# A cross-attention kernel's setup in another order: Wk's load and transposes first, batch 0's keys in pieces between the second attention's weights

## The chip, the cores and the metric

The kernel runs on one core of a Trainium2 chip. The metric is the device time in microseconds of one execution; three runs of the kernel before gave 958.2, 962.56 and 960.67, a median of 960.67. Profiles come from one further execution.

The engines are called PE (TensorE, matrix products), DVE (VectorE), ACT (ScalarE), POOL (GpSimd) and SP (SyncE, which here only issues DMAs). Each works through its own instructions in order. PE writes to PSUM, which ACT and DVE then copy to SBUF.

## What is computed

For each of 16 batches, `x` is 100 x 640 and the context is 722 x 384, of which the last four rows are the tokens `ca` and the other 718 are `enc`. There are 8 heads of 80.

```python
query = hidden_states @ Wq
keyt = enc @ Wk
valt = enc @ Wv
hs = _mha(query, keyt, valt)
ca_q1 = jnp.einsum('btc,th->bch', ca, Wq_ca)
ca_q1 = ca_q1[:, indices, :]
ca_hs1 = _mha(ca_q1, residual, residual)
ca_q2 = ca_hs1 @ Wq
ca_k2 = ca @ Wk_ca
ca_v2 = ca @ Wv_ca
ca_hs2 = _mha(ca_q2, ca_k2, ca_v2)
out = hs + ca_hs2
out = out @ Wout + b_out
out = out + residual
```

So there is a main attention over `enc`, and a second one over the four tokens whose queries come from yet another attention, of token channels over `x`. All is in 32-bit floats.

## The kernel before, in words

**The setup and the loop.** A setup loads and rearranges the weights and computes what batch 0 needs; then a loop runs over `b` in 0 to 15 (from the line `for b in range(B)`). In batch `b` the loop computes the scores of `b` (`scores`, L604), their softmax (the maxima at L1148 and L1136, `Maximum`, L1124, L1132), the values of `b` (`Values`, L425) and the keys of `b + 1` (`Keys`, L456), and at last the products of probabilities and values (L1283). From batch 1 on, keys and values come from a fast scheme with fewer products of 3 x 3 x 2 blocks, which needs sums of blocks of `enc` (`enc_sums`, on POOL, L491) and of the weights (`weight_sums`, L512). Batch 0's keys and four of its six blocks of values are computed plainly in the setup.

**The keys of batch 0.** The context's rows come in three thirds `u`, its 384 columns in three chunks `c`. `chunk_keys` (L549) computes one chunk `n` of 128 of the 640 key columns with 18 products over all thirds and chunks, and two copies by ACT (L560). `first_keys` does it for chunks 0 to 3 and then calls `last_keys` for chunk 4. The weights are Wk in rearranged columns, `wk_sb` (chunk 4: `wk4`). They are got by transposing `wkt_sb` on PE: for each `c`, three transposes into `w_ps_c` (L1037) and one copy by ACT (L1040). `wkt_sb` lies in the tile `kT`, and is loaded in five DMAs (L294), whose source `packed(wkt, c)` is 4 x 32 rows of 384 (8 x 16 for the last).

**The second attention's weights and first steps.** From `cat` and `wkca` come `k2_ps` (L991) and five masked copies (DVE, L1003); from these and the transposed Wq, `wqt` (L287, in the tile later used by Wout), the matrices `m_ps_c` (L1014), copied by DVE (L1022) to `m_sb`. `keys(load_m(b))` is five masked products on POOL (L702) into the tile `m2`. `second.products()` multiplies `m2` and `x` on PE (`y_ps`, L730) and reduces to `g` on DVE (L739). `second.scores1()` is seven POOL instructions of 100 x 800 (four products L765, three sums L772), which read `g`. `second.softmax1()` is their softmax on DVE (L656 to L686, L782); `exponentials1` is the exponential on ACT (L785). In batch 0 of the loop, `softmax1` comes ahead of the scores in DVE's order, and `exponentials1` comes between the first and the second scores' copies in ACT's order:

```python
        if b == 0:
            enc_sums(enc)
            now.load()
            now.softmax1()
        st.append(scores(b, 0, tiles))
        if b == 0:
            now.exponentials1()
        nc.vector.tensor_tensor(most[:KN], st[0][:, 0], st[0][:, 1], ALU.max)
        st.append(scores(b, 1, tiles))
        larger(1)
```

**Other pieces of the setup.** Wq is loaded in five chunks (L299) and rearranged by DVE with 15 copies (L1048, twice for each chunk, and L1055) into `wq_sb`, which the queries (L525) read. `weight_sums(nc.vector, w, False)` is seven subtractions on DVE for each of `wk_sb` and `wv_sb`; `weight_sums(nc.vector, wk_sb, True)` is five more, which overwrite raw weights and so come after batch 0's keys. `va_ps` (L1069) uses `wvca`, whose tile is the one that batch 1's `enc` is loaded to. Batch 1's `rest` is loaded to the tile that held `m_3`.

**What sets the order.** DMAs wrapped in `in_order` keep their program order on SP. From `tc.manual_schedule(engines=...)` on, every engine takes the instructions in the order of the program. Ahead of that call a planner orders each engine's instructions by its own costs, within the data's dependences; `tc.issue_after(ins)` puts a block's instructions behind a given one on its engine. In the kernel before, the call stands at the end of the setup, just ahead of the loop. So the setup is in the planner's order there, and its instructions can also stand between or behind those of the loop: Wout's load, of the loop, is issued at 38.15 us, and batch 1's `enc` at 56.05.

Of the kernel before, what the change touches and what calls it, by code (L numbers as in the profile page):

```python
# [15 lines left out]
NH, D = 8, 80  # L16
# [55 lines left out]
def packed(w, c):  # L72

    if c < 4:
        lo = (c // 2) * D + 32 * (c % 2)
        return w.rearrange("(r k) n -> r k n", r=RG)[:, lo : lo + 32]
    return w.rearrange("(h k) n -> h k n", h=NH)[:, 64:]
# [47 lines left out]
def kernel(  # L125
# [48 lines left out]
    def psum(name):  # L174

        turn[0] += 1
        return (psumk if turn[0] % 2 else psum1)(name)
# [17 lines left out]
    def vb_tile(name):  # L195
        return main.tile([P, T, H], F32, tag="vb", name=name)
# [46 lines left out]
    def in_order(dma):  # L243
        tc.keep_in_program_order(dma)
# [15 lines left out]
    def load_first(lo, hi, u, cols):  # L260

        for c in range(lo, hi):
            k = u * (KT - 1)
            in_order(
                nc.sync.dma_start(
                    out=a_raw(enc, u, c)[:, cols],
                    in_=enct[0][:, c, k + cols.start : k + cols.stop],
                )
            )
# [7 lines left out]
            )  # L277
    load_first(0, CC, 1, slice(KN, KT))
    load_first(0, CC, 2, slice(0, KT))
    tokens = vb_tile("tokens")  # L280
    cat_sb = tokens[:, CC, : CC * B * T].rearrange("p (c n) -> p c n", c=CC)
    wkca_sb = tokens[:, :CC, :]
    in_order(nc.sync.dma_start(out=cat_sb, in_=cat.rearrange("p c b t -> p c (b t)")))
    in_order(nc.sync.dma_start(out=wkca_sb, in_=wkca.rearrange("(c p) n -> p c n", p=P)))
    wqt_sb = wout_sb
    wkt_sb = kT.rearrange("p c u k -> p c (u k)")
    in_order(nc.sync.dma_start(out=wqt_sb, in_=wqt.rearrange("(c p) r -> p c r", p=P)))  # L287
    load_first(0, CC, 0, slice(0, KT))
    xT = inp.tile([P, 2, HC, S], F32, tag="xT", name="xT_0")
    in_order(nc.sync.dma_start(out=xT, in_=xt[0:2].rearrange("b p c s -> p b c s")))  # L290
    ca_0 = small.tile([S, T, S], F32, tag="ca", name="ca_0", bufs=2)
    in_order(nc.sync.dma_start(out=ca_0, in_=cas[0].unsqueeze(0).to_broadcast([S, T, S])))
    for c in range(HC):
        in_order(nc.sync.dma_start(out=wkt_sb[:, c, :CAD], in_=packed(wkt, c)))  # L294
    halves = [t[:, u] for t in [scores_tile(f"wq_{i}") for i in range(NP)] for u in range(2)]
    room = halves.pop()
    wq_in = [t[:, :H] for t in halves]
# [61 lines left out]
    def first_values(i, enc, engines, halves=(0, 1), get=psum):  # L359

        u, j = KC[i]
        for g in halves:
            engine = engines[g]
            v_ps = get(f"v_ps_0_{i}_{g}")
            for c in range(CC):
                nc.tensor.matmul(
                    v_ps[:KN, : H // 2],
                    a_raw(enc, u, c)[:, j * KN : (j + 1) * KN],
                    wv_sb[:, 2 * c + g],
                    start=(c == 0),  # L370
                    stop=(c == CC - 1),
                )
            engine(
                block(i, g)[:, :, :D],
                v_ps[:KN, : H // 2].rearrange("p (h d) -> p h d", d=D),
            )
# [167 lines left out]
    def chunk_keys(n, banks, weights, enc):  # L544
        copies = []
        for bank, thirds in zip(banks, ((0, 1), (2,))):
            for i, u in enumerate(thirds):
                for c in range(CC):
                    nc.tensor.matmul(  # L549
                        bank[:, i * KT : (i + 1) * KT],  # L550
                        weights[c],
                        a_raw(enc, u, c),
                        start=(i == 0 and c == 0),
                        stop=(c == CC - 1),
                        skip_group_check=True,
                    )
        for bank, thirds in zip(banks, ((0, 1), (2,))):
            w = len(thirds)
            copies.append(
                nc.scalar.copy(  # L560
                    kT[:, n, thirds[0] : thirds[0] + w],
                    bank[:, : w * KT].rearrange("p (u k) -> p u k", u=w),
                )
            )
        return copies

    def first_keys(enc):
        for n in range(HC - 1):
            banks = [psum(f"kT_ps_0_{n}_{k}") for k in range(2)]
            weights = [wk_sb[:, 2 * c + n % 2, n // 2] for c in range(CC)]  # L570
            chunk_keys(n, banks, weights, enc)
        last_keys(0, enc)

    def last_keys(b, enc):
        banks = pair(f"kT_ps_{b}")
        return chunk_keys(
            HC - 1,
            [banks[:, k] for k in range(2)],
            [wk4[:, c] for c in range(CC)],
            enc,  # L580
        )
# [106 lines left out]
    def load_m(b):  # L688
        if b < 2:
            return lambda c: m_sb[c][:, b * HT : (b + 1) * HT]  # L690
        mb = small.tile([P, HC, HT], F32, tag="mb", name=f"mb_{b}", bufs=2)
        nc.sync.dma_start(
            out=mb, in_=m_d[:, :, b * HT : (b + 1) * HT].rearrange("c p n -> p c n")
        )
        return lambda c: mb[:, c]
# [284 lines left out]
        nc.tensor.matmul(idle_ps[:, :P], idle, idle, start=True, stop=True)  # L980


    for i in (1, 4, 2, 5):
        first_values(i, enc, (act, dve))


    k2_ps = psum("k2_ps")
# [11 lines left out]
    for n, heads in enumerate(HEADS):  # L999
        cols = len(heads) * B * T  # L1000
        k2T.append(room[:, at : at + cols])
        at += cols
        nc.vector.tensor_tensor(  # L1003
            k2T[n].rearrange("p (h k) -> p h k", h=len(heads)),
            k2_ps[:, n * B * T : (n + 1) * B * T]
            .unsqueeze(1)
            .to_broadcast([P, len(heads), B * T]),
            hmask[:, n, : len(heads)].unsqueeze(2).to_broadcast([P, len(heads), B * T]),
            ALU.mult,
        )  # L1010
    for c in range(HC):
        m_ps = psum(f"m_ps_{c}")
        for n, heads in enumerate(HEADS):
            nc.tensor.matmul(  # L1014
                m_ps[:, heads[0] * B * T : (heads[-1] + 1) * B * T],
                wqt_sb[:, n, c * P : (c + 1) * P],
                k2T[n],
                start=(n == 0),
                stop=(n == HC - 1),
                skip_group_check=True,  # L1020
            )
        copied = nc.vector.tensor_copy(  # L1022
            m_sb[c].rearrange("p (b h t) -> p h b t", h=NH, t=T),
            m_ps.rearrange("p (h b t) -> p h b t", h=NH, b=B),
        )
        nc.sync.dma_start(out=m_d[c], in_=m_sb[c])
    second = Second(0, xT, ca_0)
    keys(load_m(0))
    summed = second.products()
    second.copy()  # L1030
    second.scores1()
    keys(load_m(1))

    for c in range(HC):
        w_ps = psum(f"w_ps_{c}")
        for cc in range(CC):
            nc.tensor.transpose(  # L1037
                w_ps[:, cc * P : (cc + 1) * P], wkt_sb[:, c, cc * P : (cc + 1) * P], ident
            )
        act(  # L1040
            wk_sb[:, c % 2 : 6 : 2, c // 2] if c < HC - 1 else wk4,
            w_ps[:, : CC * P].rearrange("p (a n) -> p a n", a=CC),
        )

    with tc.issue_after(summed.ins):
        for c in range(HC):
            for u in range(2):
                nc.vector.tensor_copy(  # L1048
                    wq_sb[:, c, 2 * u * P : 2 * (u + 1) * P].rearrange(
                        "p (a r k) -> p a r k", a=2, r=RG  # L1050
                    ),
                    wq_in[c].rearrange("p (r k) -> p r k", r=RG)[:, :, u * D : u * D + 64]
                    .rearrange("p r (a k) -> p a r k", a=2),
                )
            nc.vector.tensor_copy(  # L1055
                wq_sb[:, c, 4 * P :].rearrange("p (h k) -> p h k", h=NH),
                wq_in[c].rearrange("p (h k) -> p h k", h=NH)[:, :, 64:],
            )
    for w in wk_sb, wv_sb:
        with tc.issue_after(summed.ins):  # L1060
            weight_sums(nc.vector, w, False)
    first_keys(enc)
    weight_sums(nc.vector, wk_sb, True)

    va = wide("va")[:, : H // 2]
    va_ps = psum("va_ps")
# [11 lines left out]
    for n in range(2):  # L1078
# [1 line left out]
            out=va_d[:, n * (H // 2) : (n + 1) * (H // 2)],  # L1080
            in_=va[n * B * T : (n + 1) * B * T],
        )
    with tc.issue_after(copied.ins):
        nc.vector.tensor_reduce(
            qmask, ident.rearrange("p (r u k) -> p u r k", r=RG, u=2), AX.XY, ALU.add
        )
    tiles = queries_tiles(0)
    for n in range(HC):
        queries(0, xT, tiles, n)
    nc.gpsimd.dma_start(out=bias, in_=bout[0].partition_broadcast(P))  # L1090

    xT_at = [None]
    last, enc_next, second_next = None, load_rest(1, load_enc(1)), Second(1, xT)
    engines = {
        mybir.EngineType.Pool,
        mybir.EngineType.PE,
        mybir.EngineType.DVE,
        mybir.EngineType.Activation,
        mybir.EngineType.SP,
    }  # L1100
    ctx.enter_context(tc.manual_schedule(engines=engines))
    for b in range(B):
        p = b // 2
        e_in, now = enc, second
# [257 lines left out]
```

## Time and profile before

| | us |
|---|---|
| Median of three runs | 960.67 |
| The profiled execution, its own time | 961.78 |
| Its span in the profile | 960.1 |
| PE without work in the span | 18.0 |
| Transposes of Wk (L1037): the last nine start | 33.16 |
| Reduce to `g` of batch 0 (L739) | 29.43 |
| POOL's seven `scores1` of batch 0 (L765, L772) | 29.77 to 42.17 |
| DVE's 15 copies of Wq (L1048, L1055) | 34.86 to 43.73 |
| Keys of batch 0 on PE (L549) | 34.8 to 54.2 |
| Queries of batches 0 and 1 on PE (L525) | 55.94 to 64.66 |
| `softmax1` of batch 0 on DVE | 51.77 to 63.29 |
| Exponential of it on ACT (L785) | 68.76 to 69.64 |
| First maxima on DVE with the second scores (L1136) | 71.38 |
| PE starts again in batch 0 after its wait for DVE | 83.29 |
| PE starts in batch 1 after its wait for `enc_sums` | 125.09 |

All times count from the start of the span. An engine's row in the profile gives its busy time; an instruction that waits for another engine after it has been issued counts as busy. A group of DMA rows on SP shows when they were issued, not when the data arrived; arrival is seen in what waits for it.

### The profile page before, as it was taken

Reading aid. Unit: us, or ns where it says so; the run is one execution under the profiler, and the core shown is the slowest. Engines: PE = TensorE matmul, PEld = TensorE weight load, DVE = VectorE, ACT = ScalarE, POOL = GpSimd, SP = SyncE. Lnnn points to the kernel's source line nnn. Section 1 sums busy time; section 2 is a strip of 40 time slices with the busy share of each in tenths; the row PEclk is TensorE's granted clock in tenths of the full one; section 3 lists DMA queues with packets and bytes.
Section 4 is the critical chain, followed back from the end, with each engine's and each line's share of the span. In section 5 each row is a group of like instructions: output and inputs, shape, how many; then the busy total and the mean of one; then the engine's idle time right before and its main releaser. Section 6 shows DMA issues by size and latency. Waiting matters only on the chain.

```text
span 960.1 us, 25609 instructions
## 1 busy us (share of the span) xinstructions
PE 942.0 (98%) x11215; PEld 801.9 (84%) x11215; DVE 674.0 (70%) x1083; ACT 361.8 (38%) x598; POOL 620.1 (65%) x570
## 2 busy tenths in 40 slices
PE   9899989999999999999999999999999999999998
PEld 6797869888798798978889787898879879898866
DVE  1647686695937869496874959559694796928883
ACT  1233433434324443342434334243432444314341
POOL 4646888485955768487663958638595476845713
PEclk9999999999999999999999999999999999999999
DMA  8912105021040301204040040401204031120100
GB/s 259 293 55 69 34 17 161 3 72 58 4 146 2 94 23 51 87 1 129 1 139 12 1 129 1 135 3 44 72 1 149 2 93 37 44 86 1 59 8 29
DMA packets 45255, 62.48 MB, mean 65 GB/s; under 512 B 13336, under 2 KB 37208, under 8 KB 43544
## 3 DMA queue, kind: packets, MB, share of 16 engines
q1 hardware_dynamic: 41608, 42.97, 15.1%
q0 software_dynamic: 2512, 16.72, 6.0%
q8 instruction: 88, 1.44, 0.6%
q10 hardware_dynamic: 1024, 1.15, 0.4%
q14 instruction: 23, 0.19, 0.1%
HBM read 55.26 MB, written 5.57 MB: 63 GB/s over the span
## 4 chain that ended last, share of the span: by engine, by line
PE 91%; DMA 3%; POOL 2%; DVE 1%; issue 1%; SPq 0%; ACT 0%; ACTq 0%; DVEq 0%; POOLq 0%
PE s_ps L604 11%; PE a_ps L1283 11%; PE v_psA L425 10%; PE v_psB L425 8%; PE k_psA L456 7%; PE kT_ps L549 7%; PE q_ps L525 7%; PE o_ps L932 7%; PE k_psB L456 6%; PE v_psC L425 3%; PE k_psC L456 2%; PE v_psE L425 2%; PE v_psD L425 2%; PE y_ps L730 2%; PE k_psE L456 1%; DMA wout_sb<-in_wqt 1%
## 5 line engine op out<-in xcount | busy, mean ns | idle before, releaser
L765 POOL TENSOR_TENSOR e<-ca,g 100x800 f32<-100x800 f32 x64 | 99.3, 1561 | 142.4 <-DVE most L1136 127.9
L854 POOL TENSOR_TENSOR hs<-vb,p 100x640 f32<-100x640 f32 x64 | 105.7, 1660 | 46.7 <-DVE p L840 38.8
L861 POOL TENSOR_TENSOR hs<-hs,hs 100x640 f32<-100x640 f32 x48 | 113.8, 2372 | 3.8
L1283 PEld LDWEIGHTS a_ps<-vs,st 120*64 120x64 f32 (+3 forms) x3072 | 109.0, 125 | 5.6 <-issue 5.2
L1283 PE MATMUL a_ps<-vs,st 120*64 120x81 f32 (+3 forms) x3072 | 112.0, 234 | 0.0
L425 PE MATMUL v_psA<-wv_sb,enc 128*120 128x320 f32 x360 | 112.0, 434 | 0.0
L1124 DVE TENSOR_TENSOR st<-st,over 120x1600 f32<-120x1600 f32 x48 | 106.9, 2229 | 0.0
L491 POOL TENSOR_TENSOR enc<-enc 128x240 f32<-128x240 f32 x135 | 101.1, 763 | 7.1
L604 PE MATMUL s_ps<-qp,kT 32*120 32x100 f32 x3072 | 99.5, 265 | 1.5 <-issue 1.5
L604 PEld LDWEIGHTS s_ps<-qp,kT 32*120 32x120 f32 x3072 | 96.7, 181 | 3.2 <-issue 1.8
L621 ACT COPY st<-s_ps 120x800 f32<-120x800 f32 x64 | 49.7, 829 | 127.3 <-PE s_ps L604 127.3
L425 PE MATMUL v_psB<-wv_sb,enc 128*120 128x320 f32 x300 | 93.1, 433 | 0.0
L772 POOL TENSOR_TENSOR e<-e,e 100x800 f32<-100x800 f32 x48 | 90.5, 1886 | 3.8
L456 PE MATMUL k_psA<-enc,wk_sb 128*128 128x240 f32 x360 | 88.4, 369 | 4.4 <-POOL enc L491 2.3
L456 PEld LDWEIGHTS k_psA<-enc,wk_sb 128*128 128x128 f32 x360 | 68.4, 191 | 21.9 <-POOL enc L491 2.8
L1294 DVE RECIPROCAL rs<-a_ps 100x4 f32<-100x4 f32 x32 | 5.8, 181 | 114.9 <-PE a_ps L1283 114.9
L425 PEld LDWEIGHTS v_psA<-wv_sb,enc 128*120 128x120 f32 x360 | 64.5, 183 | 23.0 <-issue 0.5
L1132 ACT ACTIVATE st<-st 120x1600 f32<-120x1600 f32 x48 | 73.9, 1539 | 22.5 <-DVE st L1124 22.5
L1136 DVE TENSOR_TENSOR most<-most,st 120x800 f32<-120x800 f32 x64 | 66.0, 1031 | 22.4 <-ACT st L615 21.2
L491 POOL TENSOR_TENSOR enc<-enc,rest 128x240 f32<-128x240 f32 x45 | 31.8, 706 | 74.2 <-DMA rest<-in_enct 27.4
L456 PE MATMUL k_psB<-enc,wk_sb 128*128 128x240 f32 x300 | 74.7, 372 | 0.0
L425 PEld LDWEIGHTS v_psB<-wv_sb,enc 128*120 128x120 f32 x300 | 54.8, 183 | 22.1 <-DVE vs L396 0.4
(137 smaller groups left out, 1764.9 us busy)
## 6 DMA issues: line engine op xcount, KB each, us to landing
vb<-va_d POOLq DMA_DIRECT2D x16, 1000.0 KB, 7.4
enc<-in_enct SPq DMA_DIRECT2D x30, 240.0 KB
enc<-in_enct SPq DMA_DIRECT2D x15, 360.0 KB
xT<-in_xt SPq DMA_DIRECT2D x8, 500.0 KB
rest<-in_enct SPq DMA_DIRECT2D x31, 120.0 KB
xn<-in_x SPq DMA_DIRECT2D x11, 320.0 KB
out<-xn SPq DMA_DIRECT2D x11, 320.0 KB
ca<-in_cas SPq DMA_DIRECT2D x16, 156.2 KB
```

The lines of the kernel that those rows point to most:

```text
L425: nc.tensor.matmul(at[0][j][:KN, : H // 2], a_form(self.enc, f)[:, j * KN : (j + 1) * KN], wv_sb[:, W_AT[f]], start=first, stop=last, skip ...
L456: nc.tensor.matmul(at[:, i * KT : (i + 1) * KT], wk_sb[:, W_AT[f], i], a_form(self.enc, f), start=(first and i == 0), stop=last, skip_grou ...
L491: nc.gpsimd.tensor_tensor(out, left, right, op)
L525: nc.tensor.matmul(q_ps[:, : 2 * S].rearrange("p (j s) -> p j s", j=2), wq_sb[:, c, n * P : (n + 1) * P], xT[:, :, c, :], start=(c == 0), ...
L604: nc.tensor.matmul(s_ps[r][:n, 256 * a + lo : 256 * a + hi], kT[rows, c, u, j * KN : (j + 1) * KN], rhs, start=(a == 0 and c == 0), stop=( ...
L765: first = nc.gpsimd.tensor_tensor(to, self.ca[:, t, :].unsqueeze(1).to_broadcast([S, NH, S]), g[:, :, t].unsqueeze(2).to_broadcast([S, NH, ...
L772: nc.gpsimd.tensor_tensor(e, e, to, ALU.add)
L854: first = nc.gpsimd.tensor_tensor(to, vb[:S, t, :].rearrange("p (h d) -> p h d", h=NH), p2[:, :, t].unsqueeze(2).to_broadcast([S, NH, D]), ...
L861: nc.gpsimd.tensor_tensor(sums, sums, to, ALU.add)
L1124: return nc.vector.tensor_tensor(st[i], st[i], top.over[:KN].unsqueeze(1).to_broadcast([KN, 2, ROWS]), ALU.subtract,)
L1132: nc.scalar.activation(st[i], st[i], AF.Exp, scale=SCALE)
L1283: nc.tensor.matmul(a_v[lo:hi, h % 4], st[i // 2][: KEYS[i], i % 2, h * S + lo : h * S + hi], block(i, h // 4)[: KEYS[i], h % 4], start=(i ...
```

## The change

The call of `manual_schedule` moves from the end of the setup to a place ahead of the first values, so that all of the setup from there on is in program order on every engine. The program's order is rewritten:

- Wk's five loads and batch 0's `u = 0` go ahead of `cat`, `wkca`, `wqt`, `x` and the tokens.
- Wk's transposes and copies follow the first values, and `first_keys` now does one chunk per call: chunk 0 ahead of `k2_ps`, chunk 1 between `k2_ps` and `m_ps`, chunk 2 between POOL's `keys(load_m(0))` and `second.products()`, chunk 3 and `last_keys` after `va_ps`.
- `keys(load_m(1))` stands after `second.scores1()` in the program, as before; the bias's load is put between the two. In the planner's order before, both went ahead of `scores1` on POOL.
- Wq's copies, then the sums of `wk` and `wv`, follow on DVE after `second.products()` and the reduction for `qmask`.
- Batch 1's loads are asked for after `va_ps`, ahead of key chunk 3.

```diff
     load_first(0, CC, 2, slice(0, KT))
+    wkt_sb = kT.rearrange("p c u k -> p c (u k)")
+    for c in range(HC):
+        in_order(nc.sync.dma_start(out=wkt_sb[:, c, :CAD], in_=packed(wkt, c)))
+    load_first(0, CC, 0, slice(0, KT))
     tokens = vb_tile("tokens")
...
     in_order(nc.sync.dma_start(out=wqt_sb, in_=wqt.rearrange("(c p) r -> p c r", p=P)))
-    load_first(0, CC, 0, slice(0, KT))
...
-    for c in range(HC):
-        in_order(nc.sync.dma_start(out=wkt_sb[:, c, :CAD], in_=packed(wkt, c)))
...
-    def first_keys(enc):
-        for n in range(HC - 1):
-            banks = [psum(f"kT_ps_0_{n}_{k}") for k in range(2)]
-            weights = [wk_sb[:, 2 * c + n % 2, n // 2] for c in range(CC)]
-            chunk_keys(n, banks, weights, enc)
-        last_keys(0, enc)
+    def first_keys(enc, n):
+        banks = [psum(f"kT_ps_0_{n}_{k}") for k in range(2)]
+        weights = [wk_sb[:, 2 * c + n % 2, n // 2] for c in range(CC)]
+        chunk_keys(n, banks, weights, enc)
...
+    ctx.enter_context(tc.manual_schedule(engines=engines))
     for i in (1, 4, 2, 5):
         first_values(i, enc, (act, dve))
+
+    for c in range(HC):
+        w_ps = psum(f"w_ps_{c}")
...
+    first_keys(enc, 0)
...
+    first_keys(enc, 1)
     for c in range(HC):
         m_ps = psum(f"m_ps_{c}")
...
     second = Second(0, xT, ca_0)
     keys(load_m(0))
-    summed = second.products()
+    first_keys(enc, 2)
+    second.products()
     second.copy()
     second.scores1()
+    nc.gpsimd.dma_start(out=bias, in_=bout[0].partition_broadcast(P))
     keys(load_m(1))
+    nc.vector.tensor_reduce(
+        qmask, ident.rearrange("p (r u k) -> p u r k", r=RG, u=2), AX.XY, ALU.add
+    )
...
-    with tc.issue_after(summed.ins):
-        for c in range(HC):
...
     for w in wk_sb, wv_sb:
-        with tc.issue_after(summed.ins):
-            weight_sums(nc.vector, w, False)
-    first_keys(enc)
-    weight_sums(nc.vector, wk_sb, True)
+        weight_sums(nc.vector, w, False)
...
+    xT_at = [None]
+    last, enc_next, second_next = None, load_rest(1, load_enc(1)), Second(1, xT)
+    first_keys(enc, 3)
+    last_keys(0, enc)
+    weight_sums(nc.vector, wk_sb, True)
     tiles = queries_tiles(0)
     for n in range(HC):
         queries(0, xT, tiles, n)
-    nc.gpsimd.dma_start(out=bias, in_=bout[0].partition_broadcast(P))
-
-    xT_at = [None]
-    last, enc_next, second_next = None, load_rest(1, load_enc(1)), Second(1, xT)
...
-    ctx.enter_context(tc.manual_schedule(engines=engines))
     for b in range(B):
```

The numbers of instructions, DMAs and bytes stay the same.

More of the change, by code (lines that the diff above doesn't have):

```diff
@@ L285 @@
     wqt_sb = wout_sb
-    wkt_sb = kT.rearrange("p c u k -> p c (u k)")
     in_order(nc.sync.dma_start(out=wqt_sb, in_=wqt.rearrange("(c p) r -> p c r", p=P)))
-    load_first(0, CC, 0, slice(0, KT))
     xT = inp.tile([P, 2, HC, S], F32, tag="xT", name="xT_0")
@@ L980 @@
         nc.tensor.matmul(idle_ps[:, :P], idle, idle, start=True, stop=True)
+    engines = {
+        mybir.EngineType.Pool,
+        mybir.EngineType.PE,
+        mybir.EngineType.DVE,
+        mybir.EngineType.Activation,
+        mybir.EngineType.SP,
+    }
+    ctx.enter_context(tc.manual_schedule(engines=engines))
     for i in (1, 4, 2, 5):
         first_values(i, enc, (act, dve))
+    for c in range(HC):
+        w_ps = psum(f"w_ps_{c}")
+        for cc in range(CC):
+            nc.tensor.transpose(
+                w_ps[:, cc * P : (cc + 1) * P], wkt_sb[:, c, cc * P : (cc + 1) * P], ident
+            )
+        act(
+            wk_sb[:, c % 2 : 6 : 2, c // 2] if c < HC - 1 else wk4,
+            w_ps[:, : CC * P].rearrange("p (a n) -> p a n", a=CC),
+        )
+    first_keys(enc, 0)
     k2_ps = psum("k2_ps")
@@ L1021 @@
             )
-        copied = nc.vector.tensor_copy(
+        nc.vector.tensor_copy(
             m_sb[c].rearrange("p (b h t) -> p h b t", h=NH, t=T),
@@ L1028 @@
     keys(load_m(0))
-    summed = second.products()
+    first_keys(enc, 2)
+    second.products()
     second.copy()
     second.scores1()
+    nc.gpsimd.dma_start(out=bias, in_=bout[0].partition_broadcast(P))
     keys(load_m(1))
+    nc.vector.tensor_reduce(
+        qmask, ident.rearrange("p (r u k) -> p u r k", r=RG, u=2), AX.XY, ALU.add
+    )
     for c in range(HC):
[L1035 to L1038, printed above, removed]
-            )
-        act(
-            wk_sb[:, c % 2 : 6 : 2, c // 2] if c < HC - 1 else wk4,
-            w_ps[:, : CC * P].rearrange("p (a n) -> p a n", a=CC),
-        )
-    with tc.issue_after(summed.ins):
-        for c in range(HC):
[L1047 to L1058, printed above, removed]
+        for u in range(2):
+            nc.vector.tensor_copy(
+                wq_sb[:, c, 2 * u * P : 2 * (u + 1) * P].rearrange(
+                    "p (a r k) -> p a r k", a=2, r=RG
+                ),
+                wq_in[c].rearrange("p (r k) -> p r k", r=RG)[:, :, u * D : u * D + 64]
+                .rearrange("p r (a k) -> p a r k", a=2),
+            )
+        nc.vector.tensor_copy(
+            wq_sb[:, c, 4 * P :].rearrange("p (h k) -> p h k", h=NH),
+            wq_in[c].rearrange("p (h k) -> p h k", h=NH)[:, :, 64:],
+        )
     for w in wk_sb, wv_sb:
-        with tc.issue_after(summed.ins):
-            weight_sums(nc.vector, w, False)
-    first_keys(enc)
-    weight_sums(nc.vector, wk_sb, True)
+        weight_sums(nc.vector, w, False)
     va = wide("va")[:, : H // 2]
@@ L1082 @@
         )
[L1083 to L1086, printed above, removed]
+    xT_at = [None]
[3 more added lines that the diff above has]
+    weight_sums(nc.vector, wk_sb, True)
     tiles = queries_tiles(0)
@@ L1089 @@
         queries(0, xT, tiles, n)
-    nc.gpsimd.dma_start(out=bias, in_=bout[0].partition_broadcast(P))
-    xT_at = [None]
-    last, enc_next, second_next = None, load_rest(1, load_enc(1)), Second(1, xT)
[L1094 to L1100, printed above, removed]
-    ctx.enter_context(tc.manual_schedule(engines=engines))
     for b in range(B):
```

## The prediction

> **What bounds the kernel now.** I read the page first, then the chain of waits, then a table by stage and the timeline of the first 130 us, where all of the change lies.
>
> ```profile
> PE 942.0 (98%) x11215; PEld 801.9 (84%) x11215; DVE 674.0 (70%) x1083; ACT 361.8 (38%) x598; POOL 620.1 (65%) x570
> ```
>
> TensorE (PE) bounds the span as a whole: it idles 18 us of 960.1. So a new order of the setup can win idle time only, and the question is what ends last there. The chain of waits (start, length, who):
>
> ```profile
> 21.19 11.84 DMA kT<-in_wkt
> ...
> 33.16 2.07 PE w_ps L1037 x9
> 35.24 19.00 PE kT_ps L549 x90
> 54.24 1.76 PE va_ps L1069 x12
> 56.01 8.66 PE q_ps L525 x50
> 64.66 5.02 PE s_ps L604 x160
> ...
> 70.05 1.30 ACT st L615 x3
> ...
> 71.38 1.00 DVE most L1136
> ...
> 82.59 0.65 DVE kT L396
> ...
> 83.29 1.08 PE k_psA L456 x4
> ```
>
> Two hand-overs are to be seen. PE waits for Wk's load until 33.16 (3.33 us idle), then works without a gap until about 72. But from 70 to 83.3 the chain is on ACT and VectorE (DVE), and PE waits for them. Further on, the same view goes from batch 0's last values (92.5) over batch 2's load and GpSimd's (POOL's) `enc` sums to PE at 125.09, where PE waits again. So the end follows the maxima that DVE starts at 71.38, more than the end of the queries at 64.66.
>
> Wk's load, in SP's timeline (start, time over all of the row's issues):
>
> ```profile
> 22.55 5.34 SPq L299 DMA_DIRECT2D wq<-in_wq  x5
> 30.34 0.38 SPq L300 DMA_DIRECT2D wvca<-in_wvca  x1
> 33.11 2.92 SPq L1026 DMA_DIRECT2D m_d<-m  x4
> ```
>
> SP's waits say that L300 and the first L1026 each waited for a transfer of Wk; the waits fit eight transfers in flight, each issue waiting for the one eight before. So Wk's third and fourth parts landed at 30.3 and 33.1: 2.8 us for 192 KB, while the stage table (PE clock, DMA share and GB/s last) shows most DMA engines idle in such a stretch:
>
> ```profile
> 22.00:23.00 1.00, 1.00 (x10) 1.00 (x9) 0.67 (x1) 0.00 (x0) 0.00 (x0) 1.00 0.33 122
> 34.00:35.00 1.00, 1.00 (x6) 0.87 (x5) 0.14 (x1) 0.58 (x2) 0.92 (x2) 0.50 1.03 392
> ```
>
> The second row shows the price of PE's idling: a clock of 0.50 after it; rows 33 to 37 add up to 1.7 us lost. Last, DVE beside POOL:
>
> ```profile
> 34.83 1.54 POOL L765 TENSOR_TENSOR e<-ca,g 100x800 f32<-100x800 f32 x1
> 34.86 1.86 DVE L1048 COPY wq_sb<-wq 128x256 f32<-128x256 f32 x2 [5.17 <-DMA wq<-in_wq]
> ...
> 36.45 2.01 POOL L772 TENSOR_TENSOR e<-e,e 100x800 f32<-100x800 f32 x1
> 36.64 1.90 DVE L1055 COPY wq_sb<-wq 128x128 f32<-128x128 f32 x1
> ...
> 43.11 0.48 DVE L1048 COPY wq_sb<-wq 128x256 f32<-128x256 f32 x2
> ```
>
> A copy of 0.2 to 0.28 us takes up to 1.9 while POOL works, and about two pass for each POOL instruction: 8 of the 15 took from 34.86 to 42.5, beside four of them; the other 7 took 1.2 us.
>
> **What the Trainium skill says.** "SBUF — State Buffer", section "Who interferes with whom": a DVE copy in a two-port mode, or a DVE operation with two SBUF inputs, and a GpSimd instruction lock each other out for a whole instruction. The rows above agree, and so does the second kind: two maxima (L1136) took 3.22 us from 74.43 beside POOL, 2.02 from 177.82 with POOL idle. "DMA: Bandwidth & Descriptors", section "Why a DMA increments its semaphore by 16 and not by 1": a DMA runs on the largest k up to 16 that divides both slowest dimensions, on the lowest-numbered engines. Wk's parts are read as 4 x 32 rows (the last as 8 x 16), so k is 4 (8); share 0.33 at 22 us agrees.
>
> **The change part by part.**
>
> *Wk's load moved ahead.* SP issues it at 7.05, where it issued `cat`. Row 9:10 of the table (share 0.46) says that what was issued before has landed by about 9. Four parts of 2.8 us and half of one end at 9 + 11.2 + 1.4 = 21.6, say 22, by the measured spacing, on four engines. What is queued on these is late now: `u = 0` of batch 0 (360 KB at about 290 GB/s, 1.3 us) 23.3, `cat` and `wkca` (1.08 MB at 390 GB/s, 2.8) 26.2, wqt (1.64 MB, 4.2) 30.5; x, `ca`, Wq and `wvca` follow by about 41, as now.
>
> *PE's new order*, from the durations of before: first values end at 18.0; three chunks of transposes (0.6 each) 19.8; the fourth and fifth wait for Wk to 22, end 22.8; keys' chunk 0 (90 matmuls took 18.2 at full clock, 3.64 a chunk) waits for `u = 0`, 23.2 to 26.9; `k2_ps` 2.0, its masks hidden by chunk 1: 32.5; `m_ps` 6.8: 39.3; chunk 2, which hides POOL's `keys`: 43.0; `y_ps` 1.4: 44.4; g at 44.7 (29.7 before). Then va 1.8 and chunks 3 and 4: 53.5, against 55.94 now. PE's wait has shrunk by 2.4 us. Half clock after the waits near 20 and 22 is possible (0 to 1.7); I take 0 and leave 1.7 for the range.
>
> *What comes behind g on POOL and DVE is where it is paid.* POOL's seven `scores1` take 12.4 us (29.77 to 42.17), so 44.8 to 57.2. The 15 Wq copies, which lay half beside POOL and half after it, now lie wholly beside: two for each POOL instruction gives 12 in six gaps and three after the seventh: 57.7. The queries need the 13th: PE does four matmuls of the first and waits about 2.5 us, to 57.3. Queries then end at 57.3 + 7.3 + 1.7 (clock, as at 33) = 66.3.
>
> The bias DMA on POOL was issued at 11.79 in 0.57 us; now it stands behind `scores1`: 57.8. Then `keys(load_m(1))`, five of 0.3 to 0.35, which went ahead of `scores1` before. They and DVE's seven `wk` sums (2.35 together) both read two SBUF inputs and lock each other out: 57.8 + 1.7 + 2.4 = 61.9. Batch 1's rest sits in the buffer of `m_3` and can be issued by SP only after the fourth of these five, so about 61.3; two issues of 0.4 and 2 us to land: 63.8, when POOL's 13 `enc` sums (0.69 each) start; SP's later loads queue behind, needed later than this. DVE does five `wv` sums free; two and the five late `wk` sums, 0.40 each, meet the `enc` sums. No row shows a run of such sums beside POOL. From below 2.8 us (no lock), from above 7 x (0.40 + 0.69) = 7.6 (one POOL instruction between each two). I take two sums per gap, as the copies had it: 2.8 + 3.5 x 0.69 = 5.2, to 69.0. Batch 0's `softmax1` on DVE took 51.77 to 63.29 less 4.25 of waiting: 7.3. It ends at 76.3.
>
> *Who waits.* The exponential of e1 stands in ACT's order between the copies of the first and second scores. It started at 68.76, now at 76.3; behind it the second scores' copies, the maxima, and PE, whose PSUM banks these free. Shift 7.5 us. The maxima no longer meet `enc` sums (the second took 1.37 for 1.0): -0.4. PE's own stall at the queries is hidden under this. The rest to 125 us hangs on these hand-overs and shifts with it.
>
> Sum: 961.78 of the profiled execution + 7.1 = 968.9. That execution lies 1.1 above the median of 960.67, which gives 967.8.
>
> *At nothing:* qmask's reduce (0.28) stands before the first copy, which is blocked by POOL anyway; wout's and xT's later issue, as both are first read after batch 1's scores.
>
> **The rivals.**
> 1. *DVE late, by the copies alone.* The sums slip between POOL's instructions without cost: `wk`, `wv` and late sums from 57.7 take 7.2, `softmax1` 7.3: 72.2, shift 3.4, 964.1. For it: by the same section of the skill a sum shares only the read side; against: L1136 was blocked.
> 2. *Not slower: DVE stays off the path.* If the 15 copies pass beside POOL at their own 0.2 us, they end at 48, and `softmax1` starts when POOL ends `scores1`, 57.2, and ends at 64.5. The queries end at 62.2, 2.4 before now; the end 958.3. It decides where `softmax1` ends before about 66. Against it stand the 1.9 us copies.
> 3. *More than forecast.* Strict turns between sums and POOL (+2.4), and half clock early or transfers later (+1.7): 971.9.
>
> **How the numbers follow.** The forecast 0.50 (about 965.5 to 970), rival 1 0.22, rival 2 0.12, rival 3 0.16. The range 960.5 to 972.5 leaves out most of rival 2 and the far end of rival 3. 0.5% is 4.8 us, about what a measurement of this kernel tells from no change. Slower by more, above 965.5: 0.46 of the forecast, 0.16 of rival 3, 0.05 of rival 1: 0.67. Faster by more, below 955.9, would need more than all of the idle that PE has in the setup: 0.04. Within: 0.29.
>
> **What would show it.** Right: transposes of chunks 3 and 4 waiting for Wk to about 22; g near 44.7; Wq's copies of 1.5 to 1.9 us up to 57; PE idle some 2.5 us before the queries' fifth matmul; `enc` sums starting near 64 behind the load of the rest; e1's exponential released by DVE at about 76, and the maxima (L1136) 7 us later than 71.38. Wrong: copies that keep 0.28 us, ACT's exponential not waiting for DVE, or g before 41, from which on the same sum gives less than 4 us.

## The result and the profile after

The changed kernel takes 966.73 us (median of seven runs, 963.62 to 968.19) against 960.04 for the kernel before (seven runs, 958.2 to 962.56). The ratio is 1.0064, with a 95% interval of 1.0048 to 1.008: 6.1 us slower by the ratio, 6.7 by the medians. Its profiled execution took 966.73 us, of which the span is 965.0; in the profile before it was 961.78 and 960.1. So the two profiles differ by 4.9 us, a little less than the medians.

The page's row for the engines:

```profile
PE 943.9 (98%) x11215; PEld 802.3 (83%) x11215; DVE 672.4 (70%) x1083; ACT 361.5 (37%) x598; POOL 634.6 (66%) x570
```

PE has the same 11215 matmuls and is busy with them for 1.9 us more, under a lower clock; it idles for about 3 us more (21.1 of the span, 18.0 before). POOL is busy for 14.5 us more with the same 570 instructions. This is the first hint: an instruction that waits after its issue counts as busy. That the profiles differ by less than the medians is in part the clock's: the profile before has 3.4 us at a clock of 0.50 in the middle of the loop (from 681.8 us, PE busy all the time), the profile after has none there, and half of that is 1.7 us by estimate.

The lines of the changed kernel have other numbers: L995 is L1037 of before (Wk's transposes), L737 is L739 (`g`), L763 and L770 are L765 and L772 (`scores1`), L654 and L780 are L656 and L782 (the first and the last of `softmax1`), L783 is L785 (its exponential), L1060 and L1067 are L1048 and L1055 (Wq's copies), L1135 is L1136 (the maxima). In the runs further down they move by a few lines more.

The timeline of PE in the new setup shows that the wait for Wk is shorter, as planned:

```profile
18.78 1.04 PE L995 MATMUL w_ps<-ident,kT 128*128 128x128 f32 x8
20.87 0.52 PE L995 MATMUL w_ps<-ident,kT 128*128 128x128 f32 x3 [1.06 <-DMA kT<-in_wkt]
22.52 0.52 PE L995 MATMUL w_ps<-ident,kT 128*128 128x128 f32 x3 [1.12 <-DMA kT<-in_wkt]
```

Two waits of 1.06 and 1.12 us stand where one of 3.33 was. PE ends the queries at 63.03, 1.6 us ahead of before. Then it loses all of it. The groups of waits from 44 to 92 us (engine and line, what it waited for, total, times, longest):

```profile
DVE turned L654 <- POOL e L770: 8.9, 1, 8.9
ACT e L783 <- DVE e L780: 7.3, 1, 7.3
...
PE z_ps L790 <- ACT st L613: 6.4, 1, 6.4
POOL enc L491 <- DMA rest<-in_enct: 4.0, 1, 4.0
```

The first three are one chain, read from the top: DVE's `softmax1` waits 8.9 us for POOL's last `scores1`, ACT's exponential waits 7.3 us for DVE, and PE, which needs the copies behind it, waits 6.4 us. The fourth, for batch 1's `rest`, is looked at with e4. In the chain of waits this is the stretch that answers to 70 to 83.3 us of before:

```profile
73.21 1.25 DVE e L780
...
75.32 1.67 ACT st L613 x4
...
77.01 1.06 DVE most L1135
...
90.59 1.08 PE k_psA L456 x4
```

The maxima begin at 77.01 where they began at 71.38: 5.6 us late. In batch 1, PE starts after its wait for the `enc` sums at 130.80 instead of 125.09: 5.7 us late. What POOL did meanwhile, in the timelines of POOL and DVE:

```profile
45.69 12.05 POOL L763 TENSOR_TENSOR e<-ca,g 100x800 f32<-100x800 f32 x2 [3.88 <-DVE g L737]
57.83 1.94 POOL L770 TENSOR_TENSOR e<-e,e 100x800 f32<-100x800 f32 x1
```

```profile
45.72 0.48 DVE L1060 COPY wq_sb<-wq 128x256 f32<-128x256 f32 x2
...
48.41 2.44 DVE L512 TENSOR_TENSOR wk_sb<-wk_sb 128x256 f32<-128x256 f32 x7
50.76 2.91 DVE L512 TENSOR_TENSOR wv_sb<-wv_sb 128x320 f32<-128x320 f32 x7
53.57 4.46 DVE L512 TENSOR_TENSOR wk_sb<-wk_sb 128x256 f32<-128x256 f32 x5
66.94 1.01 DVE L654 STREAM_TRANSPOSE turned<-e 128x800 f32<-128x800 f32 x1 [8.92 <-POOL e L770]
```

POOL's first two products took 12.05 us where they took 3.03 before. The first alone lasted 10.37, until 56.07:

```profile
45.69 10.37 POOL L763 TENSOR_TENSOR e<-ca,g 100x800 f32<-100x800 f32 x1 [3.88 <-DVE g L737]
```

DVE's copies ran beside it at their own speed, 0.2 us apart, and the sums after them too: from 45.7 to 54.7 DVE did not pause. So the two engines did lock each other out, but it was POOL that was held.

### The profile page after: what moved, and what is told of

Read it like the earlier page. It is cut to its first block, busy times and chain, and to the rows that moved or that the text cites. A ratio compares the mean times of both kernels' runs of the same rounds, so it can differ in the third digit from the quotient of the medians.

```text
span 965.0 us, 25611 instructions
## 1 busy us (share of the span) xinstructions
PE 943.9 (98%) x11215; PEld 802.3 (83%) x11215; DVE 672.4 (70%) x1083; ACT 361.5 (37%) x598; POOL 634.6 (66%) x570
## 4 chain that ended last, share of the span: by engine, by line
PE 87%; POOL 2%; DVE 2%; issue 1%; DMA 0%; ACT 0%; SPq 0%; DVEq 0%; POOLq 0%; ACTq 0%
PE a_ps L1282 11%; PE s_ps L602 11%; PE v_psA L425 10%; PE v_psB L425 8%; PE k_psA L456 7%; PE o_ps L930 7%; PE q_ps L525 6%; PE k_psB L456 6%; PE kT_ps L549 5%; PE v_psC L425 3%; PE k_psC L456 2%; PE v_psE L425 2%; PE v_psD L425 2%; PE y_ps L728 2%; PE k_psE L456 1%; PE k_psD L456 1%
## 5 line engine op out<-in xcount | busy, mean ns | idle before, releaser
L763 POOL TENSOR_TENSOR e<-ca,g 100x800 f32<-100x800 f32 x64 | 108.4, 1705 | 140.7 <-DVE most L1135 106.0
L491 POOL TENSOR_TENSOR enc<-enc 128x240 f32<-128x240 f32 x135 | 104.2, 785 | 7.1
L770 POOL TENSOR_TENSOR e<-e,e 100x800 f32<-100x800 f32 x48 | 90.3, 1882 | 3.8
L1135 DVE TENSOR_TENSOR most<-most,st 120x800 f32<-120x800 f32 x64 | 66.6, 1041 | 22.8 <-ACT st L613 21.6
```

Source lines behind the costliest of these rows:

```text
L491: nc.gpsimd.tensor_tensor(out, left, right, op)
L763: first = nc.gpsimd.tensor_tensor(to, self.ca[:, t, :].unsqueeze(1).to_broadcast([S, NH, S]), g[:, :, t].unsqueeze(2).to_broadcast([S, NH, ...
L770: nc.gpsimd.tensor_tensor(e, e, to, ALU.add)
```

## The experiments

Each kernel was timed beside the kernel before on the same chip, so the ratios can be compared; medians between the groups of runs differ by up to 1.4 us for the same kernel. In the texts on what was expected, "the port" is what DVE and POOL lock each other out of.

| Run | What differs | Median us | Ratio to before (95% interval) |
|---|---|---|---|
| e8_control | the changed kernel, again | 966.23 | 1.0056 (1.0036 to 1.0077) |
| e1_sums_early | 14 sums moved ahead | 959.83 | 0.9998 (0.9984 to 1.0012) |
| e2_sums_copies_early | and 15 copies ahead of g | 956.56 | 0.9977 (0.9965 to 0.9988) |
| e3_reduce_first | three small reductions ahead of the copies | 964.2 | 1.005 (1.0037 to 1.0063) |
| e4_keys1_first | second `keys` ahead of `scores1` | 964.12 | 1.005 (1.0035 to 1.0066) |
| e9_keys1_first_again | the same, with e8 | 965.59 | 1.0046 (1.0029 to 1.0063) |
| e5_after_wk16 | Wk's loads on 16 engines | 961.92 | 1.0025 (1.0016 to 1.0034) |
| e6_before_wk16 | the kernel before, with that alone | 953.24 | 0.9934 (0.9913 to 0.9954) |
| e7_all_early_wk16 | e2 and e5 together | 952.93 | 0.9931 (0.9913 to 0.995) |
| e10_all_keys1 | e7 and e4 together | 952.34 | 0.9913 (0.9897 to 0.9929) |

### Taking DVE's run away: e1 and e2

The 14 early sums read raw weights only, so they can run in DVE's idle time before the masks of `k2_ps`:

```diff
     first_keys(enc, 0)
+    for w in wk_sb, wv_sb:
+        weight_sums(nc.vector, w, False)
...
-    for w in wk_sb, wv_sb:
-        weight_sums(nc.vector, w, False)
```

> Theory A (DVE's run of 15 copies and 14 sums holds the port, so POOL's first scores1 product lasts 10.4 us and softmax1 starts only at 66.9): with the 14 sums moved to DVE's idle time before k2's masks, the run after g is 2.7 us of copies; the first product lasts under 5 us, scores1 ends near 61 to 62, e1's exponential starts near 69, time about 961.5 to 962.5, 4 to 5 us under the changed kernel. Theory B (g being 16 us later than before is the whole cause, the port adds nothing): scores1 and softmax1 keep their places, time within 1 us of 966.7.

e2 also moves the loop of the 15 Wq copies to a place ahead of `second = Second(0, xT, ca_0)`, behind m's copies:

> The sums as in the run before, and the 15 Wq copies between m's copies and g. Theory A: POOL's first product lasts about 1.5 us, scores1 ends near 59, e1's exponential starts near 67, where PE and ACT end last again; the time is about 958 to 959, under the kernel before by what PE gained (1.7 us at the end of the queries). Theory B: as the changed kernel, 966 to 967.

The timelines of POOL, e1 first, then e2:

```profile
45.62 5.70 POOL L763 TENSOR_TENSOR e<-ca,g 100x800 f32<-100x800 f32 x2 [3.88 <-DVE g L737]
```

```profile
46.10 3.04 POOL L763 TENSOR_TENSOR e<-ca,g 100x800 f32<-100x800 f32 x2 [3.88 <-DVE g L737]
```

With 14 instructions less in DVE's run the two products take 5.70 us, without the run 3.04, as in the kernel before. Both have the instructions of the changed kernel and no others, and g comes at the same time (45.3 to 45.8). So theory A holds and B falls: moved away, DVE's run takes all of the loss with it. e1 came out about 2 us better than expected, and e2 1.4 us or more. What went along with it in e1 is in its stage table (PE clock, DMA share, GB/s at the end), against the same stretch of the changed kernel:

```profile
73.00:85.00 12.00, 10.42 (x92) 8.65 (x77) 10.55 (x20) 4.22 (x9) 11.60 (x11) 1.00 0.30 97
```

```profile
73.00:85.00 12.00, 7.49 (x86) 6.63 (x87) 10.12 (x12) 5.38 (x10) 11.61 (x12) 0.57 0.51 187
```

PE's wait before `z_ps` shrank from 6.36 to 1.85 us, and the mean clock of this stretch rose from 0.57 to 1.00, which the expectation had not counted. PE's busy time in the whole profile, for the same 11215 matmuls, fell from 943.9 to 940.7: 3.2 of the 6.8 us between the two profiles are the clock's, the rest is less idling. In e2 ACT's exponential no longer waits for DVE (its timeline shows it at 67.54, right behind the first scores' copies), so PE's gain at the queries comes through, and e2 is faster than the kernel before. Its profile is of its longest run, 962.11; the setup in it is read here, not its total.

### Which engine is held: e3

```diff
+    for _ in range(3):
+        nc.vector.tensor_reduce(
+            qmask, ident.rearrange("p (r u k) -> p u r k", r=RG, u=2), AX.XY, ALU.add
+        )
     for c in range(HC):
         for u in range(2):
             nc.vector.tensor_copy(
```

> Three more reductions for qmask between g and the Wq copies, so that DVE's run starts about 0.75 us later, when POOL's first product is under way. Theory C (who comes first has the port): the first product lasts about 1.5 us, the copies pass two per gap and take up to 1.9 us, the last one ends near 58, PE waits before the queries' fifth matmul, e1's exponential starts near 76 as predicted, time 967 to 969. Rival (an unbroken run on DVE wins whoever comes first): the second POOL product is held for some 9 us, copies stay at 0.28 us, time 966.5 to 968.

e3's timelines of DVE and of PE:

```profile
44.94 2.24 DVE L1064 COPY wq_sb<-wq 128x256 f32<-128x256 f32 x2
47.10 0.21 DVE L1071 COPY wq_sb<-wq 128x128 f32<-128x128 f32 x1
47.24 2.16 DVE L1064 COPY wq_sb<-wq 128x256 f32<-128x256 f32 x2
49.32 1.56 DVE L1071 COPY wq_sb<-wq 128x128 f32<-128x128 f32 x1
...
57.54 0.37 DVE L1071 COPY wq_sb<-wq 128x128 f32<-128x128 f32 x1
```

```profile
54.70 0.61 PE L525 MATMUL q_ps<-xT,wq_sb 128*128 128x200 f32 x2 [0.86 <-DVE wq_sb L1064]
57.27 3.06 PE L525 MATMUL q_ps<-xT,wq_sb 128*128 128x200 f32 x12 [1.97 <-DVE wq_sb L1064]
```

Here POOL's first product starts 1 us ahead of the first copy (43.95 against 44.94), and the roles are those of the prediction: POOL's seven instructions end at 56.58, about 12.6 us after their start; the copies pass two in a gap and end at 57.9; PE waits for the 13th until 57.27. So the rival falls, and theory C stands for a lead of 1 us; for smaller leads see the last section. The time was expected some 3 us too high, and the exponential near 76 where it started at 73.45: DVE's sums ended at 66.2, not 69, and in this profile g came 1.7 us earlier than in the changed kernel's, without a half clock near 23. The two orders cost about the same (1.005 and 1.0064, with intervals that overlap), for either way one engine stands still while the other works, and the exponential waits for both.

### The late load of batch 1's rest: e4, e9 and e10

```diff
+    keys(load_m(1))
     second.scores1()
     nc.gpsimd.dma_start(out=bias, in_=bout[0].partition_broadcast(P))
-    keys(load_m(1))
```

> keys(load_m(1)) ahead of scores1, so that batch 1's rest is loaded early and the enc sums don't wait for it at 72.9. Theory A: the end is set by softmax1 behind scores1, which now starts up to 1.6 us later; the enc sums follow scores1 without the 4 us wait; time 966.5 to 969. Theory D (the late load of the rest, with the enc sums beside the maxima, is the cause): 3 us or more faster, 962 to 964.

The first time this was 964.12, between the two expectations, so it was run again beside the changed kernel, and in e7:

> The changed kernel as it is, beside the next two on the same chip: about 966, 0.6 to 0.7% over the kernel before.

> keys(load_m(1)) ahead of scores1 in the changed kernel, a second time: the first time it came out at 1.005 of before where the changed kernel has 1.0064, with intervals that overlap. If the late load of the rest costs something of its own (theory D in part), it is 1 us or more under the control; if not, within 1 us of it or over.

> e7 with keys(load_m(1)) ahead of scores1. If the late rest costs something also where DVE has no run after g: 951.5 to 952.5, under e7's 952.9. If not: 953 to 954.5, as scores1 ends some 1.6 us later.

POOL's `enc` sums no longer wait for the rest (they start at 67.96 in e4 instead of 72.92), yet the exponential starts at 75.28 instead of 74.55. Beside its control e9 is 0.6 us faster by the medians, 1 us by the ratios. e10's median lies in the range that was set for a cost of the late rest, and its ratio is 0.0018 under e7's, which is 1.7 us. In each pair the intervals overlap, but e4, e9 and e10 all point the same way. So a share of up to about 1.7 us for the late rest stays open. It isn't the main cause: in e2 the second `keys` stands where the changed kernel has it, and the loss is gone.

### Wk on 16 engines: e5, e6 and e7

The rows of Wk's transpose are put on the host in the order of `packed`, and the parts are loaded plainly, each as 128 rows. By the rule in the prediction that is 16 DMA engines for four; it also changes the order of the rows in memory, and the two are not told apart:

```diff
-        in_order(nc.sync.dma_start(out=wkt_sb[:, c, :CAD], in_=packed(wkt, c)))
+        in_order(nc.sync.dma_start(out=wkt_sb[:, c, :CAD], in_=wkt[c * P : (c + 1) * P]))
...
-        "wkt": np.asarray(L0_xattn_Wk).T,
+        "wkt": np.asarray(L0_xattn_Wk).T[rows],
```

> The changed kernel with Wk's rows laid out on the host in the order in which the parts are read, so that each of Wk's five loads has 128 rows as its slowest dimension and runs on all 16 DMA engines. Theory E (Wk's four engines hold PE up, at the transposes and by way of wkca at k2): no PE wait of 1.06 and 1.12 us near 20.9 and 22.5 and no half clock at 23, g at 42 to 42.5 instead of 45.6, the rest shifts along, time 963 to 964. Rival (the same bytes come in the same time, the wait only moves to wkca or wqt): g at 45 or later, within 1 us of 966.7.

> The kernel before with that layout alone. Theory E: PE's wait of 3.33 us for Wk's transposes at 33.16 and the half clock after it (1.7 us) are gone; the queries end near 60 to 61; time 955.5 to 957.5, if DVE's softmax1, which ended at 63.3, moves ahead too; about 958.5 if it doesn't. Rival (another load or DVE takes its place at once): within 1 us of 960.

> Sums and copies early as in e2, and Wk on 16 engines. Theories A and E together: g near 42.5 (unless the Wq copies ahead of it wait for Wq's load until about 39 to 40), queries' end near 60, time 953 to 955. If Wq's load holds g back: 955.5 to 957.

PE's timeline in e5:

```profile
18.52 1.80 PE L995 MATMUL w_ps<-ident,kT 128*128 128x128 f32 x15
20.16 1.38 PE L549 MATMUL kT_ps<-enc,wk_sb 128*128 128x240 f32 x6
...
23.90 1.97 PE L1009 MATMUL k_ps<-tokens 128*64 128x64 f32 x60
```

All 15 transposes run without a wait, and `k2_ps` starts at 23.90 instead of 28.30, without a wait for `wkca`. g is there at 41.2, 4.4 us earlier, and the time falls by 4.8 us by the medians (1.0064 to 1.0025 by the ratios, 3.7 us). The median is 1 to 2 us under what was expected, as g had been put at 42 to 42.5. POOL's first product still lasts 10.37 us in e5, so its hold doesn't come from Wk's load. The two gains add up: one after the other, those of e2 and e5 would give 0.9938 by estimate, and e7, with both, has 0.9931.

e6 puts it into the kernel before; its chain of waits:

```profile
29.68 0.66 PE w_ps L1037 x6
...
30.36 0.98 PE w_ps L1037 x7
31.34 18.23 PE kT_ps L549 x90
```

The busy share of the DMA engines from 22 to 23 us, 0.33 before, is 1.01 here. The wait of 3.33 us until 33.16 and the half clock after it are gone, the queries end at 59.99 instead of 64.66, and the maxima start at 66.70 instead of 71.38. At 0.9934 (0.9913 to 0.9954) it beats both kernels, with the planner's order and no other edit. Its median is 2.3 us under the lowest that was expected. The expectation counted one stretch of half clock; the profile before has four of 3.4 us (from 33.3, 84.5, 125.4 and 681.8 us), that of e6 one (from 118.2), and PE's busy time falls from 942.0 to 937.0 us:

```profile
PE 937.0 (98%) x11215; PEld 797.2 (84%) x11215; DVE 672.3 (71%) x1083; ACT 361.4 (38%) x598; POOL 629.2 (66%) x570
```

So 5.0 of the 8.6 us between these two profiles are the clock's. Whether the stretch at 681.8, far from the edit, went because of it is not shown. DVE's run is there too (one of POOL's `keys` instructions, issued at 29.76, lasted 8.22 us), but `scores1` ends at 50.3 there, just before DVE's `softmax1` at 50.8, so it costs next to nothing. e7 (just under the 953 to 955 expected) and e10 reach about the same level by the order by hand (0.9931 and 0.9913): with the other layout of Wk, no gain of the new order is clear of the noise.

## Why the prediction was right, and where it was not

The forecast was 967.8 us, 7.1 us slower; measured are 966.73 and 6.1 to 6.7. The end of the chain is as it was put: DVE's `softmax1` late, ACT's exponential behind it, then the second scores' copies, the maxima and PE, all later than before while PE's own order had won time. The shift of the maxima was forecast at 7.1 and is 5.6. Step by step:

- *Wk's load.* Forecast for the fifth part about 22; the last transposes started at 22.52. In e5, with the other layout of the load, that wait is gone. `k2_ps` was put at 26.9 and started at 28.30; the half clock that the prediction left for the range came (0.66 on average from 22 to 27), and g was at 45.6 instead of 44.7.
- *The queries.* The forecast had PE waiting 2.5 us for the 13th copy and ending at 66.3. In the changed kernel PE didn't wait and ended at 63.03. This follows from the next step. e3, where the step holds, has the waits (0.86 and 1.97) and ends at 66.33.
- *The step that failed: "two for each POOL instruction", the copies to 57.7.* They ended at 48.50 without hindrance; it was POOL whose `scores1` ended at 66.9 instead of 57.2. The lock was right and the engine that is held was wrong. The prediction carried over what the lines of before show (34.83 and 34.86): the copies held, POOL not. Here the records start equally close, 45.69 and 45.72, and it is the other way round. What differs is that there POOL had been at work since 29.77 and DVE came out of a wait of 5.17 us, while here POOL came out of a wait and DVE was at work. In e4 both were at work, and POOL was held (a `keys` product for 9.10 us, from 45.82), so it isn't POOL's wait that decides; whether it is DVE's is not shown. Since `softmax1` needs both, the sum came near the truth: held copies and held sums would have let it begin at 69.0, the held POOL let it begin at 66.94. That the total came so near is in part luck. e3, where the copies are held as forecast, costs 1.0050, which is 4.8 us and not 7.1; what was too large is above all the sums' term, next.
- *The sums beside the `enc` sums (5.2 us).* That contest did not take place, for the early sums were over before. In e3, DVE's sums from 57.8 to 66.2 took 8.3 us where the prediction had 11.3.
- *`softmax1` itself* took 7.5 us for the 7.3 forecast.
- *The rest's load.* It was put at 63.8, as `keys` would stand behind `scores1`; it landed by 72.9 as `scores1` was late. (The terms given, 61.3, two issues of 0.4 and 2, add up to 64.1.) By e4, e9 and e10 it costs between nothing and about 1.7 us of its own.
- *After the maxima* the prediction let everything shift along: 5.6 there, 5.7 at batch 1's wait. In between it is no plain shift. PE starts again in batch 0 at 90.59, 7.3 us late, and its last values of batch 0 end at 98.16 for 92.54, 5.6 late; the profile before had a half clock from 84.5, the one after had it from 74.3 to 84.6. The 0.4 us for maxima that meet no `enc` sums was not won: with the rest late they met them, and three took 1.29 to 1.39 us in the chain.

Rival 2, a DVE off the path with a time of 958.3, is what e2 gives (956.56, 0.9977). It assumed copies at their own 0.2 us and took `scores1` to be unhindered at the same time. In the changed kernel the first was so and the second not.

## What to carry to other kernels

Before moving DVE work beside POOL work, look at what both read and write: here two-port copies and sums of two SBUF inputs didn't overlap with POOL's products and sums, so the later consumer pays for both, whichever of the two is held. Put such work where POOL is idle: 14 sums and 15 copies moved so took the ratio from 1.0064 to 0.9977. And before reordering transfers, see how many DMA engines each keeps busy (a share of 0.33 gave Wk's load away): another layout of one weight gave more (0.9934) than the best order tried without it (0.9977).

## What the runs showed that was not expected

A DVE run can hold POOL until its first pause: one instruction of 1.54 us lasted 10.37 while 32 copies and sums passed. The pause was of 0.03 us, between the third and the fourth of the last sums:

```profile
53.90 0.77 DVE L512 TENSOR_TENSOR wk_sb<-wk_sb 128x256 f32<-128x256 f32 x2
54.70 1.65 DVE L512 TENSOR_TENSOR wk_sb<-wk_sb 128x256 f32<-128x256 f32 x1
```

POOL's product ended 1.40 us after this pause began (54.67 and 56.07), and the fourth sum was the one that waited. In e1 and e5 it is the same: DVE's first pauses begin at 48.43 and 50.26, the products end at 49.82 and 51.66, 1.40 us later.

The Trainium skill, "SBUF — State Buffer", section "Who interferes with whom", says that whoever issues first has the shared pair for a whole instruction. In e3, with POOL 1 us ahead, that agrees: DVE was held, two copies to a gap. For smaller leads the starts in the profile don't tell who will be held. POOL is 0.03 us ahead in the kernel before, where DVE was held, and 0.03 us ahead in the changed kernel, where POOL was. In e6 it is 0.13 us ahead and is held for 8 us:

```profile
29.76 8.22 POOL L702 TENSOR_TENSOR m<-m,hmask 128x64 f32<-128x64 f32 x1 [0.25 <-PE y_ps L730]
```

```profile
29.89 0.28 DVE L1048 COPY wq_sb<-wq 128x256 f32<-128x256 f32 x1
```

Nor does the rule explain why a waiting POOL did not get its turn between two of DVE's instructions. DVE's next one starts before the last has ended (copies 0.2 us apart at 0.28 us each), which may be why; but POOL's first two products in e3 overlap as well (the second starts at 45.44, the first ends at 45.49), and there a waiting copy passed and ended at 45.64. How the turns are given stays open.
